# One operand of VectorE's dot products moved to PSUM, and a PSUM bank held for it, in a four-layer graph network on one Trainium2 core

## The chip, the cores and the metric

The kernel runs on one core of one Trainium2 chip. The metric is the device time of one execution in microseconds; lower is better. The engines are called TensorE (PE in the profile; PEld is its weight load), VectorE (DVE), ScalarE (ACT), GpSimd (POOL) and SyncE (SP, which here issues nearly all transfers). Everything is 32-bit floating point.

## The reference, cut to what matters

128 samples, each with 128 nodes of 512 features (`x`) and a 128x128 adjacency matrix (`adj`), go through four layers. After each layer the sum of its input and its result is normalised over the features. The change concerns layer 2, and layer 3 runs interleaved with it:

```python
def _L2_gnn_ref(x, A_shape, w, a):
    y = x @ w
    s = y @ a
    A = s[..., :, None] + s[..., None, :]
    A = jnp.tanh(A / 8.0) * 8.0
    A = jnp.where(A >= 0, A, 0.1 * A)
    A = jnp.exp(A) * A_shape
    A = A / jnp.sum(A, axis=-1, keepdims=True)
    A = A * jnp.sum(A_shape, axis=-1, keepdims=True)
    out = A @ x @ w
    return out
```

The score `s` of a node is the dot product of its 512 features with the vector `w @ a`. The kernel computes `w @ a` once, and then one dot product per node. Layer 3 is attention with eight heads of 64, whose scores are multiplied by twice the adjacency matrix ahead of the softmax.

## The kernel before, in words

**Tiling and stages.** Samples are handled in pairs (`U` = 2); there are 64 pairs. A tile `four` holds a pair: 128 nodes on the partitions, 2x512 features along each. Each layer is a function that is called once for two pairs (four samples) and yields between its stages: `layer0`, `layer1`, and `layer23` (line 1380), which does layers 2 and 3 together. Layer 0 and layer 1 leave their results in DRAM (`x1d`, `x2d`), and the next layer loads them. Products with the weight matrices use a Strassen scheme of seven products (`strassen`, line 630; `twice`, line 846, does two levels), whose partial results VectorE and ScalarE take out of PSUM while TensorE goes on.

**Layer 2's scores.** `park_vectors` computes `w @ a` divided by 8 and spreads it over all partitions into `wa_b` (lines 1293 and 1307), a tile of kind `row`, which lies in SBUF. In `layer23`, for each sample, `dot` (line 483) multiplies the 512 features by `wa_b` and sums into one column of `s2` (line 1394). In the trace such a dot is a SCALAR_TENSOR_TENSOR of VectorE with output `junk`, followed by a DVE_READ_ACCUMULATOR; its operands are shown as `junk<-four,row`, or with another name in place of `four`, since tiles of that kind also lie in the buffers called `out`, `first`, `side`, `rows` and `ks` once those are free. There are 128 such dots. After them TensorE transposes the spread scores (`spread_pair`, line 863), ScalarE applies tanh, the leaky slope and exp in PSUM, VectorE multiplies by the adjacency matrix, GpSimd normalises, and the matrix goes through DRAM to be transposed.

**Layer 3's scores.** `attention` (line 1469) has the score matmuls of a pair in one group (line 1477), which writes four PSUM banks. VectorE multiplies each bank by the adjacency matrix into SBUF (128x512).

**PSUM.** [...] Six are of the kind `bank` from the start (line 418), and two, `t0` and `t1`, are used apart in layer 0 and join the others after it (line 424). So layers 1 to 3 have eight. In the profile a tile in one of the first six is called `bank`, one in the last two `t`.

**The order of the work.** The kernel's calls are first collected by a planner (`Plan`), which then writes every engine's order out. Each call has a *key*, set by the stage tables (`WHEN0`, `WHENT`, `WHEN1`, `WHEN2` and others) and the number of the pair; lower keys are more urgent. `estimate` (line 124) gives a duration for each call, `shares_port` (line 151) says which calls of VectorE and GpSimd exclude each other. For VectorE's SCALAR_TENSOR_TENSOR with an accumulated output the estimate is 67 ns, 1 ns per 0.96 elements, and 118 ns if no operand lies in PSUM (line 142); such a call shares the port with GpSimd if it has two operands in SBUF.

`order` (line 239) then plays the engines in time. For each engine `look` (line 281) lists the calls whose inputs are there, and of those that can start within 60 ns of the soonest it takes the most urgent. Two of its rules matter here. SyncE's transfers without predecessors are held back until TensorE has reached a call with their key (`reached`). And a buffer is given out in the order of its tiles' keys: a tile that isn't next in line may overtake up to six others, but only if four buffers of the kind stay free beyond those that it takes (lines 296 to 300). A call that needs several new tiles, such as the group of score matmuls, starts only when all of them are to be had. The order is made three times, the second and third time with deadlines worked back from TensorE's starts (`deadlines`, line 359), and the shortest is emitted (`emit`, line 370).

Of the kernel before, what the change touches and what calls it, by code (L numbers as in the profile page):

```python
# [59 lines left out]
PE, DVE, ACT, POOL, SP = range(5)  # L60
# [17 lines left out]
class Tile:  # L78
# [3 lines left out]
    def __init__(self, kind, ap=None, place=None):  # L82
        self.kind, self.ap, self.place = kind, ap, place
        self.reads, self.writes = [], []
# [89 lines left out]
class Plan:  # L174


    def __init__(self, slots, later):
        self.slots = slots
        self.later = later
        self.key, self.late = 0, 0  # L180
        self.group = None
        self.share = 1
        self.ops = []

    def engine(self, number, real):
        plan = self
# [52 lines left out]
    def order(self, urgent=None):  # L239


        ops = self.ops
        n = len(ops)
        after = [[] for _ in range(n)]
        left = [len(o[4]) for o in ops]
        todo, first = {}, {}
        for k, o in enumerate(ops):
            for d in o[4]:
                after[d].append(k)
            for t in o[5]:  # L250
                todo[t] = todo.get(t, 0) + 1
                first[t] = min(first.get(t, o[3]), o[3])
        line = {kind: sorted((t for t in first if t.kind == kind), key=first.get, reverse=True) for kind in self.slots}
        slots = {kind: [(0, i) for i in range(m)] for kind, m in self.slots.items()}
        place = {}
        later = {new: (set(old), 0.0) for new, old in self.later.items()}

        def settle(kind):

            if line[kind] or kind not in {old[0] for olds in self.later.values() for old in olds}:  # L260
                return False
            found, slots[kind] = slots[kind], []
            for at, i in found:
                for new, (old, when) in list(later.items()):
                    if (kind, i) in old:
                        later[new] = rest, when = old - {(kind, i)}, max(when, at)
                        if not rest:
                            slots[new[0]].append((when, new[1]))
            return bool(found)

        rank = [o[3] if o[0] == PE or urgent is None else (urgent[k], k) for k, o in enumerate(ops)]
        ready = [{} for _ in range(5)]
        come, free, start = [0.0] * n, [0.0] * 5, [0.0] * n
        port = [0.0] * 5
        pipe, reached = 0.0, EARLY
        landed = [0.0] * LANES
        for k in range(n):
            if not left[k]:
                ready[ops[k][0]][k] = 0.0

        def look(e):

            can = []
            soonest = math.inf
            for k, t in ready[e].items():
                if e == SP and ops[k][8] > reached and not ops[k][4]:
                    continue
                t = max(t, free[e], port[e] if ops[k][6] else 0)
                if e == SP:
                    t = max(t, *(landed[j - LANES] - ISSUE * j for j in range(len(ops[k][1]))))  # L290
                new = {}
                for tile in ops[k][5]:
                    if tile not in place:
                        new.setdefault(tile.kind, []).append(tile)
                for kind, tiles in new.items():
                    s, m = slots[kind], len(tiles)
                    spare = 0
                    if not all(tile in line[kind][-m:] for tile in tiles):
                        spare = SPARE if all(tile in line[kind][-m - AHEAD:] for tile in tiles) else math.inf
                    if len(s) < m + (min(spare, 4) if kind == "bank" else spare):  # L300
                        break
                    t = max(t, sorted(s)[m - 1][0])
                else:
                    can.append((rank[k], t, k))
                    if t < soonest:
                        soonest = t
            if not can:
                return None
            r, t, k = min(c for c in can if c[1] <= soonest + SLACK)
            return t, k  # L310

        best = [look(e) for e in range(5)]
        count = 0
        while count < n:
            t, e = min((b[0], e) for e, b in enumerate(best) if b)
            k = best[e][1]
            o = ops[k]
            stale = {e}
            for tile in o[5]:
                if tile not in place:  # L320
                    s, l = slots[tile.kind], line[tile.kind]
                    at = min(s) if tile.place is None else next(x for x in s if x[1] == tile.place)
                    s.remove(at)
                    place[tile] = at[1]
                    l.remove(tile)
                    settle(tile.kind)
                    stale = set(range(5))
            del ready[e][k]
            start[k] = t
            free[e] = end = t + o[2]  # L330
            if o[7]:
                end = pipe = max(pipe, t + BEGIN) + o[7]
                landed += [end + LANDED] * len(o[1])
                landed = landed[-LANES:]
            if e == PE and o[8] > reached:
                reached = o[8]
                stale.add(SP)
            if o[6]:
                port[DVE + POOL - e] = end + (YIELD if e == POOL else 0)
                stale.add(DVE + POOL - e)  # L340
            count += 1
            for tile in o[5]:
                todo[tile] -= 1
                if not todo[tile]:
                    slots[tile.kind].append((end + max(LATENCY[SP if o[7] else e]), place[tile]))
                    settle(tile.kind)
                    stale = set(range(5))
            for j in after[k]:
                f = ops[j][0]
                come[j] = max(come[j], end + LATENCY[SP if o[7] else e][f])  # L350
                left[j] -= 1
                if not left[j]:
                    ready[f][j] = come[j]
                    stale.add(f)
            for f in stale:
                best[f] = look(f)
        return start, place, max(free)
# [32 lines left out]
def kernel(  # L390
# [50 lines left out]
    for kind, k, t in (*(("out", k, t) for k, t in enumerate(outs)), ("w28", 0, places["w28"][0]),  # L441
                       ("row1", 0, row1)):
        for c in range(SIZE[kind] // SIZE["four"]):
            later["four", len(places["four"])] = [(kind, k)]
            places["four"].append(t[:, c * SIZE["four"]:(c + 1) * SIZE["four"]])
    plan = Plan(slots, later)
    pe, ve, ac, po, sp = (plan.engine(*e) for e in ((PE, nc.tensor), (DVE, nc.vector), (ACT, nc.scalar),
                                                     (POOL, nc.gpsimd), (SP, nc.sync)))
# [12 lines left out]
    def bank():  # L461
        return tile_of("bank", D)
# [5 lines left out]
    def sq(n=P):  # L468
        return tile_of("sq", U, n)

    def col(*n):
        return tile_of("col", *n)
# [10 lines left out]
    def dot(dst, u, v, n=D):  # L483
        ve.scalar_tensor_tensor(junk[:, :n], u, 1.0, v, op0=OP.mult, op1=OP.mult, accum_out=dst)

    def row():
        return tile_of("row", D)
# [400 lines left out]
    WT = {}  # L888
# [404 lines left out]
    wa_b = row()  # L1293
# [86 lines left out]
    def layer23(i0):  # L1380
# [9 lines left out]
        FTs = []  # L1390
        for i, x2, A in each(both, x2s, As):
            s2 = col(U)
            for b in range(U):
                dot(s2[:, b:b + 1], x2[:, b], wa_b)
            deg = col(U)
            ve.tensor_reduce(deg, A, AX.X, OP.add)
            pt = spread_pair([s2[:, b:b + 1].to_broadcast([P, P]) for b in range(U)])
            for b in range(U):
                ac.activation(pt[:, b * P:(b + 1) * P], pt[:, b * P:(b + 1) * P], AF.Tanh, bias=s2[:, b:b + 1])
            ac.activation(pt[:, :U * P], pt[:, :U * P], AF.Prelu, alpha=0.1)  # L1400
            ac.activation(pt[:, :U * P], pt[:, :U * P], AF.Exp, scale=8.0)
            F = sq()
            r = col(U)
            for b in range(U):
                ve.scalar_tensor_tensor(F[:, b], pt[:, b * P:(b + 1) * P], 1.0, A[:, b], op0=OP.mult, op1=OP.mult,
                                        accum_out=r[:, b:b + 1])
            ve.reciprocal(r, r)
            for b in range(U):
                po.tensor_scalar(F[:, b], F[:, b], r[:, b:b + 1], deg[:, b:b + 1], op0=OP.mult, op1=OP.mult)
            FTs.append(through_dram(F.rearrange("p b (k w) -> p b k w", w=Q), f"F{i}", False))  # L1410
# [189 lines left out]
```

## Time and profile before

| what | value |
|---|---|
| median of three runs | 5381.98 us (5377.0 to 5382.57) |
| the profiled execution, its own time | 5377.98 us |
| its span, from the first instruction to the last | 5376.2 us |
| mean granted TensorE clock | 0.998 |
| TensorE busy | 5307.6 us |
| VectorE busy | 4423.1 us |
| GpSimd busy | 3906.2 us |
| ScalarE busy | 2407.2 us |
| first and last dot of layer 2 | 2967.8 us and 5225.0 us |

How to read it: busy time is the union of an engine's instructions. Instructions of VectorE follow each other with a little overlap in the records, and matmul ends are modelled, so TensorE's pace is better read from the starts of its matmuls. One matmul call gives two records in the trace (some are missing). All instructions are put down to line 381, the line that emits the planned calls, so groups are told apart by their tiles' names, output first. A wait is shown in brackets behind an instruction, with the engine and tile that ended it.

Layer 0 takes the time to about 1300 us, layer 1 to about 3000 us; the steady part of layers 2 and 3 is looked at from 3200 to 5000 us, and the end from 5000 us on.

### The profile page before, as it was taken

The page shows a single profiled execution, that of the slowest core. Times are in us where ns is not written, and L with a number is a line of the kernel's source. Part 1 is how long each engine was busy: PE and PEld are TensorE (multiplying, and loading weights), DVE is VectorE, ACT ScalarE, POOL GpSimd, SP SyncE. Part 2 cuts the span into 40 slices and gives each one's busy share as a digit, 9 for nine tenths or more (in the row PEclk, how much of TensorE's full clock was granted, in tenths as well). Part 3 has the DMA queues.
Part 4 walks back from the last instruction along what each step waited for, and adds up shares of the span by engine and source line. Part 5 has one row for each costly group of instructions (what it writes and reads, how often), then busy time and mean ns, then how long its engine had stood idle before and what let it go on. Part 6 is the DMA issues. An engine that isn't in the chain of part 4 may idle for free.

```text
span 5376.2 us, 92973 instructions
## 1 busy us (share of the span) xinstructions
PE 5307.6 (99%) x29039; PEld 4230.2 (79%) x29039; DVE 4423.1 (82%) x11721; ACT 2407.2 (45%) x6085; POOL 3906.2 (73%) x4937
## 2 busy tenths in 40 slices
PE   8999999999999999999999999999999999999998
PEld 4555555555888888888888889988998899889987
DVE  7788887887888888888888778887877888888876
ACT  3343343344544444444444344444444444444444
POOL 6777787676766666666666577777877777777776
PEclk9999999999999999999999999999999999999999
DMA  4544544445544454444444745555555455555543
GB/s 108 142 136 131 148 135 139 121 115 190 167 143 147 157 163 144 147 159 161 143 148 152 233 140 163 160 159 151 164 161 158 154 163 158 161 152 162 161 146 111
DMA packets 831143, 813.61 MB, mean 151 GB/s; under 512 B 258348, under 2 KB 631604, under 8 KB 830648
## 3 DMA queue, kind: packets, MB, share of 16 engines
q1 hardware_dynamic: 827650, 806.60, 48.9%
q8 instruction: 231, 3.78, 0.3%
q14 instruction: 264, 2.16, 0.1%
q10 hardware_dynamic: 2998, 1.06, 0.1%
HBM read 458.38 MB, written 349.04 MB: 150 GB/s over the span
## 4 chain that ended last, share of the span: by engine, by line
PE 88%; DVE 7%; issue 2%; DMA 1%; ACT 1%; POOL 1%; SPq 0%; ACTq 0%; DVEq 0%; POOLq 0%
PE bank L381 67%; PE t L381 21%; DVE four L381 2%; DVE out L381 1%; DVE col L381 1%; DVE first L381 1%; DVE junk L381 1%; POOL out L381 0%; ACT out L381 0%; DVE side L381 0%; ACT four L381 0%; DVE rows L381 0%; DVE bank L381 0%; DMA first<-in_L_gnn_Wk_dram 0%; SPq L381 0%
## 5 line engine op out<-in xcount | busy, mean ns | idle before, releaser
L381 PE MATMUL bank<-first,four 128*128 128x386 f32 (+3 forms) x6352 | 1748.6, 423 | 23.6 <-ACT first L381 9.9
L381 PEld LDWEIGHTS bank<-first,four 128*128 128x128 f32 (+2 forms) x6352 | 1089.3, 187 | 600.2 <-DVE out L381 101.9
L381 DVE TENSOR_TENSOR out<-bank,out 128x386 f32<-128x386 f32 (+1 forms) x1942 | 948.5, 507 | 253.1 <-PE bank L381 194.8
L381 DVE TENSOR_TENSOR four<-bank,four 128x256 f32<-128x256 f32 x1113 | 453.9, 416 | 151.3 <-PE bank L381 138.9
L381 POOL TENSOR_TENSOR out<-out 128x772 f32<-128x772 f32 (+3 forms) x249 | 341.6, 1381 | 272.9 <-DVE out L381 215.4
L381 POOL TENSOR_TENSOR four<-four 128x256 f32<-128x256 f32 (+2 forms) x434 | 351.5, 823 | 189.1 <-DVE four L381 140.6
L381 PE MATMUL bank<-first,out 128*128 128x256 f32 (+1 forms) x1746 | 432.4, 377 | 3.7 <-DVE four L381 1.6
L381 POOL TENSOR_TENSOR four<-four,four 128x256 f32<-128x256 f32 (+2 forms) x467 | 397.0, 855 | 10.0 <-PE bank L381 1.5
L381 POOL TENSOR_TENSOR col<-col,neghalf 128x2 f32<-128x2 f32 x320 | 227.9, 712 | 231.7 <-DVE col L381 230.5
L381 ACT COPY out<-bank 128x258 f32<-128x258 f32 (+2 forms) x489 | 194.9, 404 | 440.7 <-PE bank L381 359.9
L381 PEld LDWEIGHTS bank<-first,out 128*128 128x128 f32 (+1 forms) x1746 | 318.5, 188 | 65.4 <-issue 9.0
L381 ACT ACTIVATE four<-four,col,col 128x512 f32<-128x512 f32 (+1 forms) x355 | 308.5, 892 | 125.4 <-POOL col L381 118.9
L381 DVE TENSOR_TENSOR first<-bank,first 128x256 f32<-128x256 f32 (+1 forms) x591 | 240.4, 415 | 97.9 <-PE bank L381 89.3
L381 PE MATMUL bank<-first 128*128 128x128 f32 (+1 forms) x2132 | 297.6, 278 | 1.6 <-DVE four L381 1.6
L381 DVE BATCH_NORM_STATS2 col<-four 128x6 f32<-128x512 f32 x424 | 282.9, 681 | 10.5 <-ACT four L381 9.1
L381 ACT COPY four<-bank 128x256 f32<-128x256 f32 (+1 forms) x358 | 150.6, 424 | 303.8 <-PE bank L381 287.7
L381 PEld LDWEIGHTS bank<-first 128*128 128x128 f32 (+1 forms) x2132 | 270.0, 190 | 15.9 <-issue 4.0
L381 PE MATMUL t<-out,sq 128*128 128x512 f32 x512 | 256.3, 593 | 0.5 <-ACT t L381 0.5
L381 ACT COPY t<-out 128x512 f32<-128x512 f32 x256 | 150.9, 591 | 235.4 <-PE bank L381 73.7
L381 PE MATMUL t<-first,four 128*128 128x256 f32 (+2 forms) x1064 | 250.3, 361 | 0.6 <-DVE four L381 0.6
L381 PE MATMUL bank<-out,first 128*128 128x128 f32 (+3 forms) x1432 | 232.4, 312 | 2.2 <-DVE col L381 1.8
L381 PE MATMUL bank<-four,first 128*128 128x128 f32 (+3 forms) x1400 | 220.5, 303 | 2.4 <-DVE four L381 1.3
(526 smaller groups left out, 13149.7 us busy)
## 6 DMA issues: line engine op xcount, KB each, us to landing
h<-four SPq DMA_DIRECT2D x69, 512.0 KB, 3.3
four<-in_x_dram SPq DMA_DIRECT2D x256, 128.0 KB, 3.4
four<-h SPq DMA_DIRECT2D x64, 512.0 KB, 4.6
four<-in_x_dram SPq DMA_DIRECT2D x62, 512.0 KB, 4.5
x1d<-four SPq DMA_DIRECT2D x62, 512.0 KB, 2.9
four<-x1d SPq DMA_DIRECT2D x60, 512.0 KB, 4.5
out<-h SPq DMA_DIRECT2D x55, 512.0 KB, 5.1
h<-out SPq DMA_DIRECT2D x50, 512.0 KB, 3.2
```

Source lines behind the costliest of these rows:

```text
L381: call(*map(real, args), **{n: real(a) for n, a in kw.items()})
```

## The change

In `layer23`, the first call that comes to the scores takes a PSUM bank, `WT["a"]`, and has ScalarE copy `wa_b` into it. All 128 dots read the vector from that bank. The bank stays taken until the last dot. The copy is entered in a new set, `gated`; a call in that set is treated as SyncE's transfers without predecessors are: it isn't given to its engine before TensorE has reached its key. For this, ScalarE's choice is evaluated again too whenever TensorE reaches a new key.

By `estimate` and `shares_port`, both unchanged, a dot with an operand in PSUM has no extra 118 ns and doesn't share GpSimd's port, so the planned order of layers 2 and 3 is made anew.

```diff
@@ -181,6 +181,7 @@
         self.ops = []
+        self.gated = set()
@@ -283,7 +284,7 @@
             for k, t in ready[e].items():
-                if e == SP and ops[k][8] > reached and not ops[k][4]:
+                if ops[k][8] > reached and (k in self.gated or e == SP and not ops[k][4]):
                     continue
@@ -334,7 +335,7 @@
             if e == PE and o[8] > reached:
                 reached = o[8]
-                stale.add(SP)
+                stale |= {SP, ACT}
@@ -1390,8 +1391,12 @@
             s2 = col(U)
+            if "a" not in WT:
+                WT["a"] = bank()
+                plan.gated.add(len(plan.ops))
+                ac.copy(WT["a"], wa_b)
             for b in range(U):
-                dot(s2[:, b:b + 1], x2[:, b], wa_b)
+                dot(s2[:, b:b + 1], x2[:, b], WT["a"])
```

## The prediction

> **What bounds the kernel now.** I read the page's first part, then the table by stage for the stretch in which layers 2 and 3 run in steady state (3200 to 5000 us), then the dot products' own rows, TensorE's waits, and the timeline around one wait.
>
> ```profile
> PE 5307.6 (99%) x29039; PEld 4230.2 (79%) x29039; DVE 4423.1 (82%) x11721; ACT 2407.2 (45%) x6085; POOL 3906.2 (73%) x4937
> ```
>
> The table by stage (stretch and its length in us; busy time with instructions of TensorE, its weight loads, VectorE, ScalarE, GpSimd; clock, DMA share, GB/s):
>
> ```profile
> 3200.00:5000.00 1800.00, 1789.35 (x13260) 1621.16 (x13259) 1455.29 (x3798) 831.78 (x2819) 1396.51 (x1709) 1.00 0.52 159
> ```
>
> TensorE bounds the kernel: 1789 of 1800 us in the stage, at a granted clock of 1.00. VectorE is busy 1455 us (81%), GpSimd 1397 us (78%). So VectorE's time is worth something only where TensorE waits for it.
>
> ```profile
> L381 DVE SCALAR_TENSOR_TENSOR junk<-four,row x84: 648/710/3007, 2967.8 to 5150.2; 128x512 f32<-128x512 f32 x84
> L381 DVE SCALAR_TENSOR_TENSOR junk<-out,row x34: 677/688/1520, 3039.0 to 5190.3; 128x512 f32<-128x512 f32 x34
> L381 DVE SCALAR_TENSOR_TENSOR junk<-four,bank x8: 649/686/687, 16.7 to 24.5; 128x512 f32<-128x512 f32 x8
> ```
>
> And one row of the instructions on `bank` tiles:
>
> ```profile
> L381 DVE SCALAR_TENSOR_TENSOR four<-four,bank x49: 667/674/686, 1400.0 to 3035.9; 128x512 f32<-128x512 f32 x49
> ```
>
> These rows are min/median/max in ns. The dots of layer 2 (`row` operand) range from 648 ns to 3007 ns; the eight of the preparation, with a PSUM operand, stay within 649 to 687. Nor do 49 other instructions of this kind and width, with one SBUF and one PSUM operand, ever exceed 686, though GpSimd is busy then too (1025 of 1500 us from 1400 to 2900).
>
> ```profile
> PE bank L381 <- DVE col L381: 3.2, 15, 0.3
> PE bank L381 <- DVE four L381: 2.8, 12, 0.3
> PE bank L381 <- DVE out L381: 1.6, 7, 0.2
> PE t L381 <- DVE col L381: 1.6, 8, 0.2
> PE t L381 <- DVE out L381: 1.4, 6, 0.2
> ```
>
> All of TensorE's visible waits in the stage (10.6 us) are on VectorE. They are few but regular. One of them:
>
> ```profile
> 3314.93 1.28 POOL L381 TENSOR_TENSOR side<-ks,side 128x512 f32<-128x512 f32 x1
> ...
> 3315.26 1.50 DVE L381 SCALAR_TENSOR_TENSOR junk<-first,row 128x512 f32<-128x512 f32 x1
> ...
> 3316.56 1.03 PE L381 MATMUL bank<-out,first 128*128 128x256 f32 x4
> 3316.69 0.08 DVE L381 DVE_READ_ACCUMULATOR junk<-first,row 128x1 f32 x1
> 3316.69 0.41 DVE L381 TENSOR_TENSOR four<-t,four 128x256 f32<-128x256 f32 x1
> 3317.03 0.41 DVE L381 TENSOR_TENSOR ks<-bank,ks 128x256 f32<-128x256 f32 x1
> 3317.36 0.41 DVE L381 TENSOR_TENSOR four<-bank,four 128x256 f32<-128x256 f32 x1
> ...
> 3317.82 1.13 PE L381 MATMUL bank<-four,four 128*128 128x256 f32 x4 [0.23 <-DVE four L381]
> ```
>
> A GpSimd addition is already running when the dot starts; the dot takes 1.50 us, three evacuations queue behind it, and TensorE stands until the third is done. The idle figure, 0.23, understates it: the four matmul records before began at 3316.56 and the four before those at 3315.70, so four take 0.86 us and the next was due at 3317.42. TensorE lost 0.40 us.
>
> [...]
>
> **The change, part by part.**
>
> *Dots.* 128 of them take 138.6 us, 1083 ns on average, 64 of them above 720. At 686 each that is 87.8 us, so VectorE loses 51 us of work. Bounds: at 649 each 55 us go[...].
>
> *What of it lies on TensorE's path.* From matmul starts, 216 ns apart for 256 columns and 111 for 128 when nothing waits, I summed each spacing that exceeds its norm by over 60 ns: 12.8 us from 2950 to 3200, 57.4 to 5000, 22.9 after, 93.1 in all. For each I took the VectorE instruction that ended last ahead of it, and followed VectorE's queue back as long as it had no idle time. Where a stretched dot stands in that run, I counted the smaller of the loss and the dot's excess over 686: 1.5 + 25.4 + 5.8 = 32.7 us. It is about 1.0 us per call of the stage (four samples, 72 us), typically 0.4 us and then two of 0.1 while the weight loads catch up. The other 18 us of the 51 fall where TensorE doesn't care.
> 32.7 is a ceiling for this order of instructions: some releases will be held next by the instruction's other operand or by TensorE's own earlier result, and since the order is made anew some evacuations will be late elsewhere. I take 0.7 of it: **-23 us**. Bounds 0 and -33, to which up to -9 comes if GpSimd's instructions, blocked in turn by dots that started first, also release something.
>
> *The order.* The planner prices a dot at 718 ns now (67 + 533 + 118) and lets it wait for GpSimd's port; then at 600 without port. Real dots deviate by 365 ns before and would by 86 after, so the emitted order fits the chip better. I count no extra gain for it. Against it stands an unknown of the new order, worst at the end (TensorE idle 17.4 us of the last 376): I keep 10 us either way, estimated as about half of that. Up to some 2950 us nothing should move: the new tile and the dots come later, and evaluating ScalarE's choice once more at each key changes no choice.
>
> *The copy.* One ScalarE copy of 128x512 into PSUM; the nearest row (`t<-out`, 128x512) has 591 ns. ScalarE is busy 45%. Once: nothing. Without cover it is 0.6 us.
>
> *The gate and the wait.* The copy may go only when TensorE's plan has reached the stage's key, 128.5. Paired with the plan's order, the first matmul of that key started at 2983.0 us; the first two dots ran at 2967.8 and 2969.5. They move back some 16 us, with whatever VectorE has queued behind them if the copy were late. Their user, TensorE's transposes of the scores, ran at 2996.8, so 11 us are left: nothing; if the cover fails, a few us once. At the next pair TensorE did wait for dots (2.3 us in two waits at 3028 and 3030, one dot of 1778 ns among them), so about 1 us comes back there, within the 1.5 above.
>
> *The bank.* It is taken from about 2984 to the last dot at 5225. I paired each bank's first matmul with the end of its last reader: from 3200 to 5000 three or fewer are in use 61% of the time, six 9%, seven 4% (70 us), eight never; after 5000 eight for 2.7 us. So seven banks suffice for this order: I take 0. Lower bound 0, since a bank less can't help; upper bound 44 us, priced below.
>
> Sum: 5378.0 (span 5376.2 and 1.8 around it) - 23 = 5355. The median of the runs is 5382, 4 us above the profiled run, so I carry it over as 5382 - 23, about **5358**.
>
> **Rivals.**
> *Lost in the new order (same).* The dots shrink, but TensorE is 99% busy and its small waits move elsewhere: 5 us of 23 stay, 5377. For it: the stalls are scattered half-microseconds. Against: all visible ones are VectorE's, and they repeat with the dots.
> *The dots don't shrink (same).* If they were stretched by something else than the port, nothing is gained: 5382. The 57 PSUM rows that never stretch speak against it.
> *Banks run short (slower).* The score matmuls of `attention` take four banks in one group, and a tile may overtake the line only with four free beyond its own. With seven, three may be occupied when a group comes up, not four, and overtaking needs two or fewer in use (25% of the time) in place of three or fewer (61%). If TensorE waits for one 128x512 evacuation (0.68 us) at each of 64 groups, that costs 44 us: 5382 - 23 + 44 = 5403. It decides from 23/64 = 0.36 us per group; slower by 0.2% needs 0.53. Against it: never eight in use, and no wait on a bank shows today.
>
> **Chances.** What a measurement of this kernel can tell from no change is about 0.2%, 10.8 us. Forecast (gain of 11 to 44 us, own range 5338 to 5371) 58%; lost in the order 20% and dots that don't shrink 4%, together same 24%; banks 18%. The low end is 33 + 9 + a little: 5338. The high end takes in the same cases with the 10 us of order, and a third of the bank case: 5394; left out are some 12% above and 5% below.
>
> **What would show it.** Dots as `junk<-four,bank` with a maximum near 690 and a sum near 88 us; VectorE's busy time about 50 us less; TensorE's waits on VectorE between 3200 and 5000 down from 10.6 to some 5 us, with the stage's period below 72 us; the first 2950 us unchanged; one 0.6 us copy near 2984. I am wrong if waits "PE bank" on ScalarE or VectorE appear ahead of the 64-row score matmuls, or if the sum of TensorE's lost time stays near 93 us with short dots.

## The result, and the profile after

The changed kernel takes **5372.9 us** (median of 20 runs, 5368.7 to 5375.6) against 5380.0 us (20 runs): the ratio is 0.9987, with an interval of 0.9981 to 0.9993. It is 7 us faster where 23 were forecast. Its profiled execution took 5375.6 us, with a span of 5373.8.

Engines' busy time on the page of the changed kernel:

```profile
PE 5311.6 (99%) x29039; PEld 4239.3 (79%) x29039; DVE 4376.5 (81%) x11721; ACT 2415.8 (45%) x6086; POOL 3877.9 (72%) x4937
```

VectorE lost 47 us of work, most of what the dots gave up (52 us), and GpSimd 28 us (3906.2 to 3877.9). That these are the dots' doing too is seen in number 1 below, which changes only the dots: GpSimd's busy time falls there by 33 us (3906.2 to 3873.1). The dots of the changed kernel (min/median/max in ns, first and last start):

```profile
L382 DVE SCALAR_TENSOR_TENSOR junk<-first,bank x40: 674/678/691, 3102.1 to 5178.7; 128x512 f32<-128x512 f32 x40
L382 DVE SCALAR_TENSOR_TENSOR junk<-out,bank x34: 676/678/689, 3216.3 to 5218.5; 128x512 f32<-128x512 f32 x34
...
L382 ACT COPY bank<-row x1: 596/596/596, 2982.9 to 2982.9; 128x512 f32<-128x512 f32 x1
```

No dot of layer 2 is over 691 ns any more; their sum is 86.9 us in place of 138.6. The copy ran once, at 2982.9 us. In the stage from 3200 to 5000 us (columns as before) and in TensorE's waits there, the gain seems to be complete at first sight:

```profile
3200.00:5000.00 1800.00, 1795.00 (x13292) 1631.49 (x13291) 1422.99 (x3807) 841.77 (x2842) 1375.28 (x1712) 1.00 0.52 159
```

```profile
PE bank L382 <- DVE sq L382: 1.8, 7, 0.3
PE bank L382 <- DVE four L382: 0.6, 4, 0.2
PE bank L382 <- DVE first L382: 0.4, 1, 0.4
PE t L382 <- DVE sq L382: 0.3, 2, 0.2
PE bank L382 <- DVE out L382: 0.2, 1, 0.2
```

The visible waits fell from 10.6 to 3.3 us. But TensorE's lost time by the spacing of its matmul starts, the measure of the prediction, only fell from 57.4 to 51.2 us in this stage. The waits that the profile prints are the smaller part of it.

Where the time went is seen best by TensorE's own work. The records are paired with the emitted order, and the time is taken at which TensorE reaches a given number of its 14694 calls. Up to call 6000 both kernels are alike (2977.8 and 2978.2 us). After that, in the profiled executions, us:

| kernel | calls 6000 to 6800, the start of layer 2 | 6800 to 13000, steady | 13000 to the last |
|---|---|---|---|
| before | 257.0 | 1673.1 | 459.7 |
| changed | 264.3 | 1666.7 | 456.0 |

It gains 6 us in the steady part and 4 at the end, and gives 7 back at the start of layer 2. The two executions differ by 2.4 us, less than the medians' 7: that of the changed kernel is the slowest of its 20. At the start of layer 2 two stops of 2 us stand out in the changed kernel's timeline, neither of which the kernel before has:

```profile
3100.82 1.41 PE L382 MATMUL bank<-sq,four 128*128 128x128 f32 x5 [2.01 <-issue]
...
3135.28 1.01 PE L382 MATMUL t<-four,first 128*128 128x128 f32 x3 [2.04 <-DVE first L382]
```

Each of them costs more than its 2 us. Behind both the trace shows a granted TensorE clock of about one half (0.51 and 0.52; columns as before; the kernel before has 1.00 in both stretches), and eight matmuls of 128 columns take 1.91 us there, where those just ahead of the first stop take 1.16:

```profile
3100.00:3107.00 7.00, 6.18 (x29) 6.21 (x30) 4.57 (x18) 1.17 (x2) 5.19 (x8) 0.51 0.00 0
3134.00:3141.00 7.00, 5.72 (x27) 5.72 (x28) 3.26 (x10) 3.16 (x14) 5.56 (x4) 0.52 0.49 154
```

```profile
3102.65 1.91 PE L382 MATMUL t<-sq,four 128*128 128x128 f32 x8
```

In these stretches the matmuls start 213 ns apart, not 111. With 29 and 27 such spacings that is an estimated 3 us behind each stop, so the two stops make some 10 us in all, more than the 7 that the changed kernel gives back here.

### The profile page after: what moved, and what is told of

Read it like the earlier page. It is cut to its first block, busy times and chain, and to the rows that moved or that the text cites. A ratio compares the mean times of both kernels' runs of the same rounds, so it can differ in the third digit from the quotient of the medians.

```text
span 5373.8 us, 92844 instructions
## 1 busy us (share of the span) xinstructions
PE 5311.6 (99%) x29039; PEld 4239.3 (79%) x29039; DVE 4376.5 (81%) x11721; ACT 2415.8 (45%) x6086; POOL 3877.9 (72%) x4937
## 4 chain that ended last, share of the span: by engine, by line
PE 87%; DVE 7%; ACT 2%; issue 2%; DMA 1%; POOL 1%; SPq 0%; ACTq 0%; DVEq 0%; POOLq 0%
PE bank L382 65%; PE t L382 21%; DVE out L382 2%; DVE four L382 2%; DVE col L382 1%; DVE first L382 1%; ACT out L382 1%; DVE side L382 1%; SPq L382 0%; DVE sq L382 0%; DVE rows L382 0%; ACT four L382 0%; ACT t L382 0%; POOL four L382 0%; ACT bank L382 0%
## 5 line engine op out<-in xcount | busy, mean ns | idle before, releaser
L382 POOL TENSOR_TENSOR out<-out 128x772 f32<-128x772 f32 (+3 forms) x248 | 342.9, 1392 | 264.3 <-DVE out L382 205.9
L382 PE MATMUL bank<-first,out 128*128 128x256 f32 (+2 forms) x1956 | 444.9, 366 | 3.3 <-DVE four L382 1.6
L382 POOL TENSOR_TENSOR col<-col,neghalf 128x2 f32<-128x2 f32 x320 | 227.6, 711 | 256.8 <-DVE col L382 255.0
L382 PEld LDWEIGHTS bank<-first,out 128*128 128x128 f32 (+2 forms) x1956 | 329.2, 183 | 66.3 <-issue 10.4
L382 ACT ACTIVATE four<-four,col,col 128x512 f32<-128x512 f32 (+1 forms) x303 | 265.7, 906 | 134.4 <-POOL col L382 127.4
L382 PE MATMUL bank<-out,first 128*128 128x128 f32 (+3 forms) x1724 | 286.8, 305 | 3.2 <-DVE rows L382 0.7
L382 PE MATMUL bank<-four,first 128*128 128x256 f32 (+2 forms) x1392 | 287.9, 340 | 0.9 <-DVE four L382 0.5
L382 DVE TENSOR_TENSOR four<-t,four 128x256 f32<-128x256 f32 x459 | 190.7, 419 | 87.4 <-PE t L382 79.2
L382 PE MATMUL bank<-first 128*128 128x128 f32 (+2 forms) x1852 | 253.5, 278 | 3.2 <-DVE four L382 1.3
L382 PEld LDWEIGHTS bank<-out,first 128*128 128x128 f32 (+2 forms) x1724 | 238.2, 189 | 22.3 <-DVE four L382 2.7
L382 DVE BATCH_NORM_STATS2 col<-four 128x6 f32<-128x512 f32 x372 | 246.5, 680 | 9.4 <-ACT four L382 9.1
L382 ACT COPY four<-bank 128x256 f32<-128x256 f32 (+1 forms) x308 | 132.5, 432 | 257.0 <-PE bank L382 222.8
L382 PEld LDWEIGHTS bank<-first 128*128 128x128 f32 (+2 forms) x1852 | 227.5, 185 | 19.8 <-DVE four L382 5.0
```

Source lines behind the costliest of these rows:

```text
L382: call(*map(real, args), **{n: real(a) for n, a in kw.items()})
```

## The experiments

Four questions, in turn: what the short dots are worth in the order of before; whether the new order costs; whether the bank or the price makes the new order; through which rule.

**1. The old order with short dots.** The order is planned as before. When it is written out, 126 of the dots get another operand, and PSUM's tiles are given out anew among seven banks (that part of the edit is left out here).

```diff
         for k in line:
+            if k == self.dots[0]:
+                self.fill(held)
             for call, args, kw in self.ops[k][1]:
-                call(*map(real, args), ...)
+                args = [held if k in self.swap and x is self.vector else real(x) for x in args]
+                call(*args, ...)
```

> Every engine's order is that of the kernel before; only the dots read the vector from a PSUM bank (126 of 128), and the tiles of PSUM are given out anew among the seven banks left. Theory A (the stretched dots cost 33 us of TensorE's time at most, and the new order gave back what was gained): 5350 to 5362 us, TensorE's lost time from 3200 to 5000 us down from 57 to some 35 us. Theory B (TensorE's stalls stand on other things, short dots gain some 6 us in any order): about 5373 us.

Measured: 5350.1 us (5349.0 to 5350.3), ratio 0.9946 (0.9933 to 0.9958): **27 us faster** than before (5377.3 in the same series), 23 faster than the changed kernel. TensorE's lost time from 3200 to 5000 us is 37.1. The place whose timeline the prediction showed now reads, in this kernel:

```profile
3314.86 1.29 POOL L388 TENSOR_TENSOR side<-ks,side 128x512 f32<-128x512 f32 x1
...
3315.43 0.68 DVE L388 SCALAR_TENSOR_TENSOR junk<-first,bank 128x512 f32<-128x512 f32 x1
...
3316.03 0.42 DVE L388 TENSOR_TENSOR four<-bank,four 128x256 f32<-128x256 f32 x1
3316.37 0.41 DVE L388 TENSOR_TENSOR ks<-t,ks 128x256 f32<-128x256 f32 x1
3316.73 1.03 PE L388 MATMUL bank<-out,first 128*128 128x256 f32 x4
...
3316.93 0.42 DVE L388 TENSOR_TENSOR four<-bank,four 128x256 f32<-128x256 f32 x1
...
3317.60 1.67 PE L388 MATMUL bank<-four,four 128*128 128x256 f32 x7
```

The same GpSimd addition runs, the dot takes 0.68 us beside it, and the matmuls follow 0.87 us after the four before them, without a wait. Theory A holds for the dots: the loss was theirs. How much of the 27 us came through VectorE, and how much through GpSimd, whose busy time is 33 us less here, is not told apart.

**2. The new order with long dots.** As the changed kernel, with the operand of the dots put back when the order is written out (the edit is shown in part).

```diff
+                if k in self.swap:
+                    args = [self.vector if x is self.copied else x for x in args]
                 call(*map(real, args), ...)
```

> The order of the changed kernel, its copy and its held bank included, but the dots read the vector from SBUF as before. Theory A (the new order costs what the short dots gain): 5388 to 5396 us, against 5380 before. Theory B (the order costs nothing): about 5380 us, 7 above the changed kernel.

Measured: 5389.4 us, ratio 1.0021 (1.0014 to 1.0029): 12 us slower than before. So the new order is worse with either kind of dot: by 12 us with long ones, by 23 with short ones (5372.9 against 5350.1). The start of layer 2 takes 264.7 us here, as in the changed kernel, and TensorE's two longest waits there are again 2.0 and 3.0 us: they belong to the order.

**3. Meant as a ceiling.** The old order with dots over 8 of the 512 features; the rest of the scores' sum is left out.

```diff
+                if k in self.dots:
+                    args = [x[:, :8] if isinstance(x, View) and x.idx.size > 8 else x for x in args]
```

> The order of the kernel before with dots over 8 of the 512 features from SBUF (the rest of the scores' sum is left out), so that nearly all of the dots' 139 us leaves VectorE: a ceiling for what shorter dots can gain in that order. Theory A: 5340 to 5352 us. Theory B: 5365 us or more.

Measured: 5348.7 us, ratio 0.9944 (0.9931 to 0.9956), 29 us faster than before. But it isn't the ceiling that the expectation tells of. The dots still have two operands in SBUF, and they are still stretched:

```profile
L384 DVE SCALAR_TENSOR_TENSOR junk<-four,row x84: 123/162/2548, 2967.8 to 5125.2; 128x8 f32<-128x8 f32 x84
```

49 of the 128 take over 720 ns, and their sum is 62.3 us, not nearly nothing. Against an undisturbed 0.162 us each, an estimated 42 us of stretching are left, of 51 before (138.6 less 128 times 0.681). So this kernel takes away most of the dots' work and little of their stretching, number 1 the stretching and none of the work, and both gain nearly the same: the two runs don't tell stretching from work. What this one shows is that about 25 us less of VectorE's time than in number 1 (62.3 against 87.8) are worth 1.4 us more. Here too GpSimd's busy time fell by 34 us.

**4. The bank, first try.** The dots planned and run from SBUF, with the copy, the gate and, to the end, the bank.

```diff
             for b in range(U):
-                dot(s2[:, b:b + 1], x2[:, b], WT["a"])
+                dot(s2[:, b:b + 1], x2[:, b], wa_b)
+            if i + U >= B:
+                ac.copy(junk[:, :1], WT["a"][:, :1])
```

> The order is planned with the copy, the gate and the held bank, but with dots that are planned and run from SBUF, so that only the bank's loss is new (one ScalarE copy of one column at the end keeps the bank). If the bank's loss costs: 5386 us or more, with the loss of the changed kernel between 2978 and 3240 us seen here too. If seven banks suffice: 5377 to 5383 us.

Measured: 5377.6 us, ratio 0.9999 (0.9991 to 1.0007). This didn't try what it was meant to. The trace has the first copy at 2986.1 us and the second, which should have kept the bank to the end, at 2986.8: it needs nothing but the first, so the planner ran it at once. The rest of TensorE's order is that of the kernel before, so what it does show is that the copy and the gate cost nothing.

**5. The bank, kept.** The second copy is gated too (`plan.gated.add(len(plan.ops))` ahead of it).

> As the run with the held bank, mended: there the copy that was to keep the bank to the end ran at once (0.7 us after the first), so only copy and gate were tried. Here it waits for TensorE's last key, so the bank is really taken from 2984 us on; the dots are planned and run from SBUF. Theory C (the bank's loss in planning makes the longer order): 5386 to 5393 us. Theory D (the dots' new price and port make it): 5375 to 5381 us.

Measured: 5379.0 us, ratio 1.0001 (0.9993 to 1.0010). With long dots the lost bank costs nothing in sum: theory C missed here, and theory D's 5375 to 5381 us was met. By parts, the start of layer 2 takes 261.4 us, 4 more than before, and the end gives as much back.

**6. The price, first try.** Eight banks in the planning, the dots priced as in the change:

```diff
                 dot(s2[:, b:b + 1], x2[:, b], wa_b)
+                plan.ops[-1][2] -= 118
+                plan.ops[-1][6] = False
```

> The order is planned with eight banks but with the dots' new price (600 ns) and without the port, then the dots read from PSUM and the tiles are given out among seven banks as in the first run. Theory C: 5347 to 5356 us, as with the old order. Theory D: 5368 us or more, as the changed kernel.

Measured: 5386.8 us, ratio 1.0016 (1.0009 to 1.0023). It isn't the kernel that the expectation tells of: where the order has eight banks in use at once, seven can't be given out, and with that only 2 of the 128 dots came to read from PSUM. It is an order made for short dots, run with long ones, and 8 us slower than before.

**7. Bank and price apart, with short dots.** Two kernels complete the square: the changed kernel with the old price (`plan.ops[-1][2] += 118`, `plan.ops[-1][6] = True` after each dot), and number 6 with the giving out begun after the first two dots, so that 126 read from PSUM.

> The changed kernel, but its planner prices the dots as before (718 ns, with GpSimd's port); seven banks. Theory C (planning with a bank less makes the worse order, at any price): 5365 to 5375 us, no better than the changed kernel's 5373. Theory D (the price makes it): 5350 to 5358 us, the old order's 5350 and some 5 us that the bank costs between 2978 and 3240 us.

> Planned with eight banks and the dots' new price (600 ns, no port), and this time 126 of the 128 dots (all but the first two) read from PSUM; before, only 2 did, since the giving out of seven banks stopped at the first moment with eight in use. Theory C: 5347 to 5358 us. Theory D: 5362 us or more.

Measured: 5360.5 us, ratio 0.9967 (0.9954 to 0.9979), and 5351.4 us, ratio 0.9950 (0.9936 to 0.9964). All four with short dots, medians in us:

| dots from PSUM | priced 718 ns with port | priced 600 ns, no port |
|---|---|---|
| planned with eight banks | 5350.1 | 5351.4 |
| planned with seven banks | 5360.5 | 5372.9 (the change) |

With eight banks in the planning the price costs 1 us, which the intervals don't tell from nothing. The bank costs 10 us at the old price and 22 at the new. The first kernel, at 5360.5, lies between both theories; the second, at 5351.4, lies where theory C had it.

The same square with long dots is on record as well, and it looks different:

| dots from SBUF | priced 718 ns with port | priced 600 ns, no port |
|---|---|---|
| planned with eight banks | 5377.3 to 5380.0 (before) | 5386.8 (number 6, all but two dots) |
| planned with seven banks | 5379.0 (number 5) | 5389.4 (number 2) |

With long dots it is the price that costs, 7 to 10 us, and the bank 0 to 3. So the bank's cost is not a sum that comes on top of any kernel. Short dots gain 27 and 35 us in the orders planned with eight banks, and only 16 to 19 in those planned with seven (the orders of a pair are the same, those of numbers 5 and 7 nearly so): what the lost bank takes is a part of the dots' gain.

**8. The rule.** Two edits of the overtaking rule, one in the changed kernel and one in the eight-bank kernel of number 7:

```diff
-                    if len(s) < m + (min(spare, 4) if kind == "bank" else spare):
+                    if len(s) < m + (min(spare, 3 if reached >= 128 else 4) if kind == "bank" else spare):
```

```diff
-                    if len(s) < m + (min(spare, 4) if kind == "bank" else spare):
+                    if len(s) < m + (min(spare, 4) + (reached >= 128) * (spare > 0) if kind == "bank" else spare):
```

> The changed kernel, but from key 128 on (layer 2) a tile of PSUM may overtake with three banks free beyond its own, not four, so that with seven banks overtaking is allowed at the same number of banks in use as before with eight. If theory C works through the overtaking rule: 5345 to 5358 us. If it works through the score matmuls' group of four banks, which still finds one bank less: 5365 us or more.

> Planned with eight banks and the new price, dots from PSUM (all but the first two), as in the run of 5351 us; but from key 128 on overtaking needs five banks free beyond its own, so that it is allowed at just the number of banks in use at which seven banks and four allow it. If the overtaking rule is the whole of the bank's cost: 5366 to 5378 us, as the changed kernel's 5373, with calls 6000 to 6800 of TensorE (the start of layer 2) some 264 us long. If the bank counts by itself (the groups of four): 5349 to 5358 us.

Measured: three spare banks with seven give **5352.8 us**, ratio 0.9953 (0.9940 to 0.9966), within 1.5 us of eight banks and 20 faster than the change. Five with eight give 5382.0 us, ratio 1.0006 (0.9997 to 1.0014), 31 slower than four with eight, and 4 us above the range of 5366 to 5378 that was written for the rule. TensorE's waits in the first of these, from 3200 to 5000 us, are down to one line:

```profile
PE bank L382 <- DVE first L382: 0.2, 1, 0.2
```

and the second has the two stops of the changed kernel at the start of layer 2 again (waits from 2950 to 3250 us, kernel with eight banks and five spare):

```profile
PE bank L388 <- DVE first L388: 2.8, 2, 2.0
PE bank L388 <- issue: 2.0, 1, 2.0
```

By parts, in us:

| kernel | 6000 to 6800 | 6800 to 13000 | 13000 to the last |
|---|---|---|---|
| eight banks, four spare (7) | 253.1 | 1657.8 | 453.1 |
| seven banks, four spare (the change) | 264.3 | 1666.7 | 456.0 |
| seven banks, three spare | 255.0 | 1658.9 | 451.4 |
| eight banks, five spare | 259.2 | 1669.3 | 468.5 |

So the rule alone, with no bank taken in the planning, makes a loss of about the same size in the first two parts (6 + 12 us, against 11 + 9), and loosening it by the one bank undoes nearly all of it. The 15 us at the end of the last kernel are its own; the change has 3 there, and the miss of the range comes from them (its profiled execution is the slowest of its 13, 4 us above their median). In the first part the two kernels without the loss have no wait over 0.9 us and a granted clock of 1.00; the one with five spare has both stops, but a half clock behind only one of them, and for half as long (a mean clock of 0.99 from 2950 to 3250 us, against 0.98 in the changed kernel).

The planner foretold most of this. The end that `order` returns for the emitted order, the planner's own estimate, is 5276.7 us for the kernel before and for eight banks at the new price, 5292.9 for the change and 5292.7 for seven banks at the old price, 5273.3 for three spare with seven and 5302.9 for five spare with eight. The bank's cost stands in it as 16 us; the price's 12 us do not. With long dots it foretells less: it is 5294.1 us for number 5, which is no slower than before.

**9. A price in between.** The changed kernel with dots at 680 ns (`plan.ops[-1][2] += 80`).

> The changed kernel with the dots priced at 680 ns, without port. With seven banks 600 ns gave 5373 us and 718 ns with the port 5360 us. If a price below the real 677 ns makes the order worse on the chip: 5358 to 5364 us. If the price only turns out another order, by chance as good or bad, there is no telling: anywhere from 5355 to 5380 us, and a value outside 5358 to 5364 speaks for that.

Measured: 5367.0 us, ratio 0.9980 (0.9971 to 0.9988), outside 5358 to 5364. By what was written, that speaks for chance. Yet the three values with seven banks fall in line, 5372.9 at 600, 5367.0 at 680, 5360.5 at 718 with port.

**10. No spare banks.** The rule taken away for PSUM in the whole kernel (a tile may still overtake no more than six), at the new price and at 718 ns without port:

```diff
-                    if len(s) < m + (min(spare, 4) if kind == "bank" else spare):
+                    if len(s) < m + (0 if kind == "bank" and spare < math.inf else spare):
```

> The changed kernel with no spare bank asked for overtaking (up to six places) in the whole kernel. If the rule costs TensorE time wherever it binds, this is faster than every kernel so far: 5320 to 5340 us, with part of the gain ahead of 2978 us. If it protects against worse orders: 5370 us or more.

> No spare bank asked for overtaking, as in the run of 5346 us, and the dots priced at 718 ns (no port). If a price near the real cost (677 ns and the accumulator's read) makes the order fit the chip better: 5330 to 5342 us. If the price doesn't matter: 5343 to 5349 us.

Measured: 5345.7 us, ratio 0.9940 (0.9927 to 0.9953), 5 to 6 us above what was expected, and **5339.2 us**, ratio 0.9928 (0.9915 to 0.9940). Both are faster than before and than the change; the second, 39 us faster than before, is the best of the study. About 4 us of each come ahead of call 6000 (2974.2 and 2974.5 us), so the rule costs little in layers 0 and 1. The planner's own ends are 5254.3 and 5255.1 us.

## Why the prediction was wrong, step by step

- **The dots shrink to 686 ns, 87.8 us in all: right.** 677 or 678 ns in the median and 86.9 us.
- **What of it lies on TensorE's path: right in mechanism, a little low.** I took 23 us, 0.7 of a ceiling of 32.7. In the order for which it was worked out it was 27 us (number 1). The stall that the timeline showed vanished at its place. That the rest of the dots' time doesn't matter to TensorE fits number 3, where about 25 us more off VectorE brought 1.4.
- **The copy and the gate, nothing: right.** 0.596 us once at 2982.9 us; number 4 shows no cost. The first 2950 us are unchanged.
- **The bank, 0, "seven banks suffice for this order": the step that failed, together with "I keep 10 us either way" for the order.** The sentence is true: number 1 runs this order in seven banks. But the planner doesn't keep the order. It makes it anew under a rule that counts free banks, and with one bank less the rule blocks overtaking far more often. The order that results costs 23 us with short dots, more than twice the 10 that I kept for it. I had named the rule in the rival on banks and had counted its base (61% of the time against 25%), but priced only a wait of the score matmuls' group for an evacuation.
- **The rival on banks: right in the place, wrong in the form and too large.** What counts is not a wait on a bank in the trace, but matmuls that the planner put in a worse order. It cost 10 to 22 us, not 44, and so the sign held.
- **The sum.** -27 for the dots, +22 for the bank with the new price and +1 for the price alone make -4, against the 7 us that were measured; the medians of the kernel before differ by as much between the two series (5377.3 and 5380.0). In my own sum 5382 less 23 is 5359, not 5358.
- **What would show it: partly a bad test.** The visible waits fell below the 5 us that I named, without the gain. The lost time by spacing did tell: in the steady stage it only fell from 57.4 to 51.2. Not foreseen at all was the half clock behind the two stops, an estimated 6 us.

Here the shortage of banks shows as scattered stops, which the trace puts down to VectorE or to "issue" (2.04 and 2.01 us for the two at the start of layer 2); no row says that a bank was missing.

Open is why the price costs 12 us with seven banks and 1 with eight. The higher price gave the faster kernel in each comparison with seven banks (numbers 7, 9 and 10). That it lies nearer to the real cost is not shown: a dot's record has 677 ns, but in the changed kernel the instruction behind its accumulator read starts 604 ns after the dot in the median (0.60 us in the timeline of number 1), which is nearer to 600 than to 718. An order made greedily can also change by several us for any small cause, and no run tells the two apart. Open too is which of the tiles that may no longer overtake cost the time, and why the bank costs next to nothing with long dots.

## What to carry to other kernels

When an order is made by rules that count free buffers, taking a buffer has two prices: waiting for it, which a count of buffers in use can exclude, and the orders that the rules no longer allow, which no profile of the old order shows. The planner's own estimate of the new order can show a part of it before anything runs, as the 16 us did here. Change the rule by the same amount as the buffers, or hold the order fixed, and the two come apart. What is lost in this way need not show in every kernel: here it was a part of what short dots gain, and with long ones it was not there. And where one engine is busy 99% of the time, take its lost time from the spacing of its starts: here the printed waits fell by two thirds (10.6 to 3.3 us) while the loss hardly moved (57.4 to 51.2 us).

## What the runs showed of the hardware that was not expected

With two operands, one of them in PSUM, the dots took 677 or 678 ns, where the prediction had 686 from the eight of the preparation; that is 4 less than the undisturbed 681 from SBUF (median of the 64 dots of the kernel before that took no more than 720). GpSimd's work got shorter with these dots too: its busy time fell by 28 us with the same 4937 instructions, and by 33 in number 1. In the kernel before, one of its TENSOR_TENSORs of 128x512 that started during a dot, at 4359.29 us, took 1.75 us, where the mean of the 143 of that size with the tiles `four<-four,four` is 1.28. And a stop of 2 us of TensorE was followed, both times at the start of layer 2 in the changed kernel, by a granted clock of one half, for 6.8 us each (0.50 from 3100.2 and from 3134.3 us); in number 2, whose order is the same, for 3.4 us. How long a stop has to be for that is not shown: in the kernel before TensorE waited up to 1.5 us between 2950 and 3250 us with the clock at 1.00, but near its end the clock was at one half for 3.4 us each (0.51 from 5155.1 us, 0.50 from 5329.2) behind stops of 1.79 and 1.28 us.
